# One set in four of a selective scan takes delta*u*B from TensorE; states outside channels; the convolved map is streamed

## The chip, the cores and the metric

The kernel runs on one core of a Trainium2 chip. The metric is the device time of one execution in microseconds (us), lower is better. Three executions of the kernel before took 12178.32, 12185.96 and 12192.31 us. All data are float32.

A NeuronCore has engines that each work through an instruction queue of their own, in order: TensorE (PE, with its weight loads PEld), VectorE (DVE), ScalarE (ACT), GpSimd (POOL) and the sync engine (SP), which issues most DMA transfers. They hand work to each other by semaphores. On-chip data lie in SBUF (128 partitions) and in PSUM (128 partitions, eight banks of 512 float32 a partition).

## The reference, cut to what matters

Two image layers run one after the other on 8 images of 64 x 64 positions and 96 channels. Each is a group norm, an input projection to 192 inner channels and 192 gates, a 3x3 depthwise convolution, a state-space scan with 16 states per inner channel, a norm with a gate, an output projection, and a residual. In the first layer the scan runs in four directions (by row, by column, and both backward):

```python
def _selective_scan(u, delta, A, Bs, Cs, D, delta_bias):
    delta = softplus(delta + delta_bias[None, :, None])
    def step(h, inp):
        u_t, d_t, B_t, C_t = inp        # B_t, C_t: 16 states, the same for all channels
        dA = exp(d_t[..., None] * A)
        h = dA * h + d_t[..., None] * B_e * u_t[..., None]
        return (h, sum(h * C_e, axis=-1))
    _, ys = lax.scan(step, h0, (u_l, d_l, B_l, C_l))
    return moveaxis(ys, 0, -1) + u * D[None, :, None]

xs = _cross_scan(xc)                    # 4 directions of the convolved map xc
x_dbl = einsum('bkdl,kcd->bkcl', xs, x_proj_w)
dts, Bs, Cs = x_dbl[:, :, :R], x_dbl[:, :, R:R+N], x_dbl[:, :, R+N:]
dts = einsum('bkrl,kdr->bkdl', dts, dt_projs_w)
y = _selective_scan(xs, dts, -exp(A_logs), Bs, Cs, Ds, dt_projs_b)
```

So for each channel c, state s and position t the scan needs a decay exp(delta[c,t] A[c,s]), a drive delta[c,t] u[c,t] B[s,t], a linear recurrence over t, and a sum over s of h C[s,t].

## The kernel before, in words

**Tiling.** For each image the first layer's scan is cut into 16 *units*: 4 directions x 4 stretches of T = 1024 positions. A unit has two *jobs*, one for each half of 96 inner channels. A job has three *groups* of 32 channels, and a group has four *sets*, i = 0 to 3, of 4 states. A set is one tile of 128 partitions (32 channels x 4 states) by 1024 positions. That makes 384 sets an image and 3072 in all, 256 jobs of 12 sets. From the second image on, six *short* sets for the other layer (on the ends of the map alone) hang on the end.

**One set** takes these steps. In brackets is the engine and the line:
- `fill` (ACT, L940): the decay, exp(scale * dt), into a PSUM tile of the pool `pslot`, which has two slots.
- `advance_set` (DVE): the product of the group's `drive` (delta*u, copied to PSUM by ACT in L957) and the replicated B (L974), then the recurrence, a tensor_tensor_scan (L987), into a `set` tile. For set i = 3 the product is made early on POOL from SBUF (`early`, L964), and DVE makes the scan alone.
- `keep_state` (ACT, L998): the last column is kept for the next stretch.
- `read_out` (POOL, L1003): `out` = `set` times the replicated C.
- `collect` (PE, L1039): four matmuls by `w_gather` sum the four states into `acc`, one PSUM bank for a group, four quarters of 256 positions on four blocks of 32 partitions. Ahead of set 0, four matmuls (L1030) begin the sums with what `y` holds from the directions before, or with the skip term for the first direction.
- `release` (ACT, L1069): after the group's last set, four copies bring `acc` back to the map `y`. The pool `pacc` has one slot: a group's first matmul waits for the release of the group before.

**The order is written out by hand** in `scan_rows`. A loop over n = the number of the set on DVE issues for each step, in this order: the loads (`fetch` of dt and dtu for the group five sets on, `replicate` of B and C for the unit four sets on), `advance_set(n)`, `keep_state(n-1)`, `fill(n+1)`, `drive(n+2)`, `release(n-4)`, `read_out(n-1)`, `early(n+2)`, `collect(n-3)` and the stages of a *plan* for this step. In the steps with (n+1) % 4 == 0 the stages come before `collect`. The program keeps this order on every engine (`tc.manual_schedule()`).

**The plan** spreads other work over the steps: for the job two ahead, its deltas (`ready_by_time`: matmuls L694 for the argument, ACT for softplus, transposes back by L728, the copy L740, the product delta*u on POOL, L606, and the store to DRAM, L616); for the unit two ahead its projection (L576); and the convolutions of the next image's first layer and of the last image's second (`conv_beside`, L1106). All of these share one PSUM bank (`pmisc`, one slot), so each stage on PE waits for the ACT copy of the stage before.

**Layouts.** In a set, the four states of a channel lie on adjacent partitions (`rep` is loaded by one DMA of 32 channels x 4, with the state index inner). The convolved map `xc` (two tiles of 32 KB a partition in `keep`: this one, and y) stays in SBUF for the whole scan; the next one is written to DRAM by `conv_beside` and loaded by `next_map` in four pieces at the end.

The lines that the change touches most:

Of the kernel before, what the change touches and what calls it, by code (L numbers as in the profile page):

```python
# [16 lines left out]
L = HH * WW  # L17
# [14 lines left out]
HALF = 2 * (T // P) * C  # L32
# [20 lines left out]
def two_ss2d_layers(ctx: ExitStack, tc: tile.TileContext, t: dict, out: bass.AP):  # L53
# [16 lines left out]
    keep = ctx.enter_context(tc.tile_pool(name="keep", bufs=2))  # L70
# [47 lines left out]
    w["skip0"] = const.tile([C, NH, C], F32, name="skip0")  # L118
    for h in range(NH):
        nc.vector.tensor_scalar(  # L120
            w["skip0"][:, h, :], w["eye"], w["dsum0"][:, h : h + 1], None, ALU.mult
        )

# [264 lines left out]

    def like(ap, by_column):

        return ap.rearrange("p (a b) -> p a b", b=HH) if by_column else ap
# [39 lines left out]
    def scan_rows(xc, y, parts, plan, rows, beside):  # L431
# [10 lines left out]
        with (  # L442
            tc.tile_pool(name="loads", bufs=2, side="right") as loads,
            tc.tile_pool(name="piece", bufs=1) as piece,
            tc.tile_pool(name="work", bufs=2) as work,
# [8 lines left out]
            with tc.manual_schedule():  # L454
                state = None
                arena = piece.tile([P, 4 * T], F32, name="arena")
                plan.setdefault(-1, []).insert(0, lambda: low_rows(x_dbl, units[1], rows))
                for n in range(-AHEAD, max(total + 4, max(plan, default=0) + 1)):
                    at = lambda i: sets[n + i] if 0 <= n + i < total else None
                    m, j = divmod(n + 1, PER)  # L460
                    if j == 0 and 0 <= m < len(jobs):

                        stages = []
                        if m + 2 < len(jobs):
                            prepare = short_ready if jobs[m + 2]["unit"]["short"] else ready_by_time
                            stages += prepare(xc, x_dbl, jobs[m + 2], arena, pmisc)
                        if m % NH == 1 and m // NH + 2 < len(units):
                            unit = units[m // NH + 2]
                            project = short_projection if unit["short"] else projection
                            stages += project(xc, x_dbl, unit, rows, pmisc)  # L470
                        for step, stage in stages:
                            plan.setdefault(n + step, []).append(stage)
                    fetch(at(AHEAD), False, loads)
                    fetch(at(2), True, loads)
                    replicate(at(AHEAD_BC), x_dbl, loads)
                    replicate_short(at(AHEAD_BC), "b", loads)
# [5 lines left out]
                    fill(at(1), pslot)  # L482
                    drive(at(2), False, pdrive)
# [6 lines left out]
                    if not late:  # L490
                        collect(at(-3), xc, y, pacc)
                    for stage in plan.pop(n, []):
                        stage()
                    if late:
                        collect(at(-3), xc, y, pacc)
# [23 lines left out]

    def ring(s):  # L520
        return s["unit"].get("ring", 2 * NS + 1)

    def fetch(s, short, loads):
# [1490 lines left out]
```

## Time and profile before

| | |
|---|---|
| three runs | 12178.32 / 12185.96 / 12192.31 us |
| profiled execution, its own time | 12189.28 us |
| its span, first to last instruction | 12187.5 us |
| busy: PE / weight loads / DVE / ACT / POOL | 72% / 33% / 89% / 74% / 86% |
| mean granted TensorE clock | 0.77 |
| DMA | 1862 MB, 153 GB/s on average |
| DVE scans, L987 | x3072, 2344 or 2286 ns each |
| DVE products, L974 | x2352, 1199 ns |
| POOL readout, L1003 / early product, L964 | x3120, 2361 ns / x768, 2414 ns |

A row of the profile names the source line, the engine, the operation, output and inputs by the program's names, the shapes and the count; then the group's busy time in us and the mean of one in ns; then the idle time of the engine just before these instructions, and what ended most of it. The timeline gives start and length in us. Where a row of the stretches between two times is shown, each engine has its busy time and its number of instructions.

### The profile page before, as it was taken

The page shows a single profiled execution, that of the slowest core. Times are in us where ns is not written, and L with a number is a line of the kernel's source. Part 1 is how long each engine was busy: PE and PEld are TensorE (multiplying, and loading weights), DVE is VectorE, ACT ScalarE, POOL GpSimd, SP SyncE. Part 2 cuts the span into 40 slices and gives each one's busy share as a digit, 9 for nine tenths or more (in the row PEclk, how much of TensorE's full clock was granted, in tenths as well). Part 3 has the DMA queues.
Part 4 walks back from the last instruction along what each step waited for, and adds up shares of the span by engine and source line. Part 5 has one row for each costly group of instructions (what it writes and reads, how often), then busy time and mean ns, then how long its engine had stood idle before and what let it go on. Part 6 is the DMA issues. An engine that isn't in the chain of part 4 may idle for free. (4 is left out here: it accounts for less than half of the span.)

```text
span 12187.5 us, 147673 instructions
## 1 busy us (share of the span) xinstructions
PE 8804.0 (72%) x50996; PEld 4018.9 (33%) x50996; DVE 10891.5 (89%) x6819; ACT 9067.0 (74%) x14930; POOL 10497.4 (86%) x4748
## 2 busy tenths in 40 slices
PE   5775577777777777776777777777687776876567
PEld 2332233332333323333233332333233332333222
DVE  6999889997999979999799997999979998899985
ACT  4777777777777777777778777787777777777775
POOL 3999889996999969999699986999879998799973
PEclk7776677778777887778877778777787777877667
DMA  3444444445444444444444444444544444444441
GB/s 96 166 153 156 138 161 155 160 163 153 153 161 164 164 142 165 153 160 160 144 167 163 164 151 155 163 155 160 174 131 165 164 164 156 146 150 158 159 142 59
DMA packets 670707, 1862.42 MB, mean 153 GB/s; under 512 B 186728, under 2 KB 201486, under 8 KB 669949
## 3 DMA queue, kind: packets, MB, share of 16 engines
q1 hardware_dynamic: 662781, 1840.30, 45.4%
q10 hardware_dynamic: 7168, 12.59, 0.3%
q8 instruction: 405, 6.64, 0.2%
q14 instruction: 353, 2.89, 0.1%
HBM read 1539.34 MB, written 313.28 MB: 152 GB/s over the span
## 5 line engine op out<-in xcount | busy, mean ns | idle before, releaser
L1003 POOL TENSOR_TENSOR out<-set,c_rep 128x1024 f32<-128x1024 f32 x3120 | 7305.7, 2361 | 826.4 <-PE acc L1039 329.8
L987 DVE TENSOR_TENSOR_SCAN set<-decay,state,set 128x1024 f32<-128x1024 f32 x2304 | 5360.5, 2344 | 350.5 <-ACT decay L940 112.6
L940 ACT ACTIVATE decay<-dt_rep,w_a 128x1024 f32<-128x1024 f32 x3072 | 3424.0, 1115 | 430.3 <-DVE set L987 428.9
L974 DVE TENSOR_TENSOR set<-drive,b_rep 128x1024 f32<-128x1024 f32 x2352 | 2819.2, 1199 | 26.3 <-ACT drive L957 16.0
L1039 PE MATMUL acc<-out,w_gather 128*32 128x256 f32 x24576 | 2384.5, 516 | 6.8 <-POOL out L1003 6.7
L1106 PE MATMUL ps_conv<-edged,taps 96*96 96x512 f32 (+1 forms) x4032 | 2198.5, 688 | 10.9 <-ACT arena L706 8.3
L964 POOL TENSOR_TENSOR set<-dtu_rep,b_rep 128x1024 f32<-128x1024 f32 x768 | 1853.7, 2414 | 89.5 <-DMA dt_far<-arena 39.1
L987 DVE TENSOR_TENSOR_SCAN set<-decay,set 128x1024 f32<-128x1024 f32 x768 | 1743.0, 2286 | 140.3 <-ACT decay L940 47.9
L728 PE MATMUL ps_sp<-w_eye,arena 128*96 128x128 f32 x7680 | 1162.0, 316 | 712.1 <-ACT arena L740 679.7
L1030 PE MATMUL acc<-map,w_eye 96*32 96x256 f32 x4608 | 577.1, 584 | 1359.0 <-ACT map L1069 1092.3
L1069 ACT COPY map<-acc 32x256 f32<-32x256 f32 x3072 | 1471.3, 479 | 66.2 <-PE acc L1039 25.8
L728 PEld LDWEIGHTS ps_sp<-w_eye,arena 128*96 128x96 f32 x7680 | 1005.7, 147 | 1017.6 <-ACT arena L740 795.1
L1039 PEld LDWEIGHTS acc<-out,w_gather 128*32 128x32 f32 x24576 | 878.3, 140 | 1382.9 <-issue 1072.0
L998 ACT COPY state<-set 128x1 f32<-128x1 f32 x2304 | 433.1, 188 | 1070.4 <-DVE set L987 1062.4
L694 PE MATMUL ps_dt<-w_dtw,x_dbl 7*128 7x96 f32 x3840 | 798.1, 370 | 498.7 <-ACT arena L740 423.1
L1106 PEld LDWEIGHTS ps_conv<-edged,taps 96*96 96x96 f32 (+1 forms) x4032 | 701.3, 189 | 1276.1 <-issue 1186.0
L694 PEld LDWEIGHTS ps_dt<-w_dtw,x_dbl 7*128 7x128 f32 x3840 | 695.3, 267 | 743.6 <-ACT arena L740 496.6
L957 ACT COPY drive<-dtu_rep 128x1024 f32<-128x1024 f32 (+1 forms) x816 | 816.5, 1001 | 33.5 <-DVE x_in L1651 13.5
L705 ACT ACTIVATE arena<-ps_dt 128x384 f32<-128x384 f32 x480 | 235.9, 492 | 620.8 <-PE ps_dt L694 597.4
L1030 PEld LDWEIGHTS acc<-map,w_eye 96*32 96x32 f32 x4608 | 104.1, 125 | 1679.8 <-ACT map L1069 1304.3
L606 POOL TENSOR_TENSOR arena<-arena,map 96x1024 f32<-96x1024 f32 x240 | 635.4, 2647 | 12.0 <-ACT arena L740 12.0
L576 PE MATMUL ps_proj<-map,w_wx 96*78 96x512 f32 x512 | 405.9, 931 | 13.7 <-ACT z L640 9.6
(202 smaller groups left out, 7682.4 us busy)
## 6 DMA issues: line engine op xcount, KB each, us to landing
dt_rep<-dt_far SPq DMA_DIRECT2D x768, 512.0 KB
dtu_rep<-dtu_far SPq DMA_DIRECT2D x768, 512.0 KB
b_rep<-x_dblr SPq DMA_DIRECT2D x256, 512.0 KB
c_rep<-x_dblr SPq DMA_DIRECT2D x256, 512.0 KB
b_rep<-x_dblc SPq DMA_DIRECT2D x256, 512.0 KB
c_rep<-x_dblc SPq DMA_DIRECT2D x256, 512.0 KB
dt_far<-arena SPq DMA_DIRECT2D x240, 384.0 KB
dtu_far<-arena SPq DMA_DIRECT2D x240, 384.0 KB
```

Of the source, the lines that this page charges most:

```text
L694: nc.tensor.matmul(job["ps"][:, j, :], unit["x_dbl"][: R + 1, at : at + P], w["dtw0"][:, k, h * C : (h + 1) * C], start=True, stop=True,)
L728: nc.tensor.matmul(job["ps"][:C, j * P : (j + 1) * P], job[name][:, s * BLOCKS + j, :], w["whole_eye"], is_transpose=True, start=i == 0, s ...
L940: nc.scalar.activation(s["decay"], s["group"]["dt"], AF.Exp, scale=rate)
L957: nc.scalar.copy(s["group"]["drive"], s["group"]["dtu"])
L964: nc.gpsimd.tensor_tensor(s["buf"], s["group"]["dtu"], b, ALU.mult)
L974: nc.vector.tensor_tensor(s["buf"], s["group"]["drive"], b, ALU.mult)
L987: nc.vector.tensor_tensor_scan(ordered(s["buf"], unit), ordered(s["decay"], unit), ordered(s["buf"], unit), 0.0 if unit["nth"] == 0 else s ...
L1003: nc.gpsimd.tensor_tensor(s["out"], s["buf"], s["unit"]["c", s["i"]], ALU.mult)
L1030: nc.tensor.matmul(acc, lhs[:, GC * g : GC * (g + 1)], positions(old[:, h, :], unit["column"], unit["t0"] + at, n), start=True, stop=False ...
L1039: nc.tensor.matmul(acc, w["gather"], s["out"][:, at : at + n], start=False, stop=s["i"] == NS - 1, skip_group_check=True,)
L1069: nc.scalar.copy(yk, like(acc, unit["column"]))
L1106: nc.tensor.matmul(job["ps"][:C, :], taps[l][:k, h, tap, :], edged[:k, tap // 3 : tap // 3 + rows, tap % 3 : tap % 3 + WW], start=tap == 0 ...
```

## The change

**Set 1 of each group on TensorE.** For i = 1 the product with B on DVE goes. TensorE makes delta*u*B straight into a PSUM slot of `pslot`: for each block of 64 positions and each of the four states, delta*u turned (positions on the partitions, 32 channels) is multiplied by a 64 x 64 block that has B on its diagonal and zeros elsewhere. Blocks of the first and second half of the 1024 positions lie on partitions 0 to 63 and 64 to 127, so 8 blocks x 4 states x 2 halves = 64 matmuls write the tile. The scan reads its source from there. The decay of set 1 goes to a tile in SBUF, since the slot is taken.

**The diagonals** are made in DRAM: two buffers are zeroed once, and for each unit four DMAs write the 4 x 1024 values of B, element by element, on the diagonals (`spread_diagonal`, 24 sets ahead). They are loaded in four parts, two DMAs each (`load_diagonal`). B of set 1 is no longer replicated.

**delta*u turned.** `turning` transposes a job's delta*u in eight matmuls and two ACT copies. delta*u is now kept in the order of these blocks, and its store to DRAM takes two DMAs.

**Who multiplies what else.** POOL's early product moves from set 3 of every group to set 0 of the first and third group of a job. DVE multiplies set 0 of the second group, set 2 and set 3.

**States outside.** In a set the four states are now the outer index of the partitions (32 channels, four times), so each replicated load becomes four DMAs of 32 partitions. The ring for B and C has 8 slots in place of 9, dtu has one slot in place of two, and is fetched one step later. `drive` is copied in step n-1 in place of n-2.

**The map is streamed.** The convolved map no longer stays in SBUF: it is stored twice in DRAM, by row and by column (`store_maps`, five DMAs a piece), and each unit loads its 1024 positions (`load_u`). The skip term is made by ACT into `y` (`skip_term`) in place of the first matmuls' weights. `next_map` is gone.

**Steps of the plan.** The deltas' stages stand at other steps by half (`late`), the convolution's nine matmuls are issued three at a time in every job.

The diff, cut to its core:

```diff
+RB = P // 2
+NR = HALF // RB        # 8 blocks of 64 in a half
+BY_PE = 1
+RING = 2 * NS
...
+    def store_maps(b, h, at, v):
+        far, far_col = xc_far[b]
+        nc.sync.dma_start(far[:, h, at], v)
+        rows = slice(at.start // WW, at.stop // WW)
+        for q in range(NT):
+            dst = far_col[:, h, q * T : (q + 1) * T].rearrange("p (a b) -> p a b", b=T // HH)
+            nc.sync.dma_start(dst[:, rows, :], by_piece(v)[:, q])
+    def load_u(b, unit):
+        unit["u"] = upool.tile([C, NH, T], F32, name="u")
+        nc.sync.dma_start(unit["u"], xc_far[b][unit["column"]][:, :, t0 : t0 + T])
+    def skip_term(unit, h, y):
+        nc.scalar.mul(y[:, h, t0 : t0 + T], unit["u"][:, h, :], w["dsum0"][:, h : h + 1])
...
-                    fetch(at(AHEAD), False, loads)
-                    fetch(at(2), True, loads)
+                    fetch(at(AHEAD), ("dt",), False, loads)
+                    fetch(at(AHEAD - 1), ("dtu",), False, loads)
+                    fetch(at(2), ("dt", "dtu", "cum"), True, loads)
                     replicate(at(AHEAD_BC), x_dbl, loads)
+                    spread_diagonal(at(2 * PER), x_dbl)
+                    head = sets[0] if n == -AHEAD else at(2 * NS - 1)
+                    load_diagonal(head, range(1), diagonals)
+                    load_diagonal(at(NS - 1), range(1, PARTS), diagonals)
...
                     advance_set(at(0), state, work)
                     keep_state(at(-1))
-                    fill(at(1), pslot)
-                    drive(at(2), False, pdrive)
+                    product_by_pe(at(1), pslot)
+                    fill(at(1), pslot, work)
+                    drive(at(1), False, pdrive)
                     drive(at(1), True, pdrive)
                     release(at(-4), y, beside)
...
+    def load_channels(rep, src):
+        for s in range(GS):
+            nc.sync.dma_start(rep[GC * s : GC * (s + 1)], src)
...
+    def spread_diagonal(s, x_dbl):
+        for i in range(GS):
+            dst = bass.AP(tensor=whole.tensor, offset=whole.offset + i * RB,
+                ap=[[2 * NR * GS * RB + 1, RB], [GS * RB, 2 * NR], [1, 1]])
+            src = x_dbl[unit["k"] % 2][row + i, unit["t0"] : unit["t0"] + T]
+            nc.sync.dma_start(dst, src.rearrange("(b r) -> r b", r=RB).unsqueeze(2))
...
+    def product_by_pe(s, pslot):
+        s["drive"] = pslot.tile([P, T], F32, name="decay")
+        turned, at = group["job"]["turned"], slice(GC * group["g"], GC * (group["g"] + 1))
+        for b in range(NR):
+            for i in range(GS):
+                for h in range(2):
+                    rows = slice(RB * h, RB * (h + 1))
+                    start = HALF * h + RB * b
+                    nc.tensor.matmul(
+                        s["drive"][GC * i : GC * (i + 1), start : start + RB],
+                        turned[rows, b, at],
+                        s["unit"]["diagonal", b // n][rows, b % n, i, :],
+                        start=True, stop=True, skip_group_check=True)
...
+    def by_pe(s):
+        return s["i"] == BY_PE and not s["unit"]["short"]
     def by_gpsimd(s):
-        return s["i"] == NS - 1
+        return s["i"] == 0 and s["group"]["g"] != 1 and not s["unit"]["short"]
...
+        if by_pe(s):
+            s["decay"] = work.tile([P, T], F32, name="decay_far", bufs=1)
+            nc.scalar.activation(s["decay"], s["group"]["dt"], AF.Exp, scale=rate)
+            return
...
-            b = unit["b", s["i"]]
-            nc.vector.tensor_tensor(s["buf"], s["group"]["drive"], b, ALU.mult)
+            if by_pe(s):
+                source = s["drive"]
+            else:
+                b = unit["b", s["i"]]
+                nc.vector.tensor_tensor(s["buf"], s["group"]["drive"], b, ALU.mult)
+                source = s["buf"]
...
             ordered(s["decay"], unit),
-            ordered(s["buf"], unit),
+            ordered(source, unit),
```

## The prediction

> **What bounds the kernel now.** I read the page's shares first, then the costliest groups, then the busy time of one inner stretch, then the waits and the timeline of one group.
>
> ```profile
> PE 8804.0 (72%) x50996; PEld 4018.9 (33%) x50996; DVE 10891.5 (89%) x6819; ACT 9067.0 (74%) x14930; POOL 10497.4 (86%) x4748
> ...
> L1003 POOL TENSOR_TENSOR out<-set,c_rep 128x1024 f32<-128x1024 f32 x3120 | 7305.7, 2361 | 826.4 <-PE acc L1039 329.8
> L987 DVE TENSOR_TENSOR_SCAN set<-decay,state,set 128x1024 f32<-128x1024 f32 x2304 | 5360.5, 2344 | 350.5 <-ACT decay L940 112.6
> L940 ACT ACTIVATE decay<-dt_rep,w_a 128x1024 f32<-128x1024 f32 x3072 | 3424.0, 1115 | 430.3 <-DVE set L987 428.9
> L974 DVE TENSOR_TENSOR set<-drive,b_rep 128x1024 f32<-128x1024 f32 x2352 | 2819.2, 1199 | 26.3 <-ACT drive L957 16.0
> L964 POOL TENSOR_TENSOR set<-dtu_rep,b_rep 128x1024 f32<-128x1024 f32 x768 | 1853.7, 2414 | 89.5 <-DMA dt_far<-arena 39.1
> L1069 ACT COPY map<-acc 32x256 f32<-32x256 f32 x3072 | 1471.3, 479 | 66.2 <-PE acc L1039 25.8
> ```
>
> Over the whole span DVE is busy 89% and POOL 86%, but that mixes the row scans with the phases between images. The row scan alone, in 1000 us of the second image (busy us of PE, PEld, DVE, ACT, POOL, then clock, DMA share and GB/s):
>
> ```profile
> 1700.00:2700.00 1000.00, 758.03 (x4708) 364.00 (x4706) 963.12 (x553) 775.29 (x1287) 946.51 (x405) 0.78 0.48 165
> ```
>
> DVE has 4% idle and POOL 5%: both bound it, TensorE and ACT do not. Per job (12 sets, three groups of four; 256 jobs) DVE works 12 scans x 2.33 (mean of both forms of L987) + 9 products x 1.20 (L974) + 0.58 for the convolution's curve = 39.3 us, and 96.3% busy makes that 40 to 41 us a job. What TensorE waits for, since it is about to get work that DVE waits for:
>
> ```profile
> PEld acc L1030 <- ACT map L1069: 1572.8, 351, 12.7
> ...
> PE ps_dt L694 <- ACT arena L740: 423.1, 232, 3.1
> ```
>
> TensorE's queue stands behind ACT: the first matmul of a group's accumulation (L1030) waits until ACT has copied the previous group's sums out of the one PSUM bank (L1069). Where in time that lies, at the end of a job (start, length in us):
>
> ```profile
> 2406.64 4.59 DVE L987 TENSOR_TENSOR_SCAN set<-decay,state,set 128x1024 f32<-128x1024 f32 x2
> ...
> 2409.12 1.11 ACT L940 ACTIVATE decay<-dt_rep,w_a 128x1024 f32<-128x1024 f32 x1
> 2410.26 1.49 ACT L1069 COPY map<-acc 32x256 f32<-32x256 f32 x4
> 2411.15 1.20 DVE L974 TENSOR_TENSOR set<-drive,b_rep 128x1024 f32<-128x1024 f32 x1
> 2411.78 0.58 ACT L740 COPY arena<-ps_sp 96x512 f32<-96x512 f32 x1
> ...
> 2412.41 1.13 PE L694 MATMUL ps_dt<-w_dtw,x_dbl 7*128 7x96 f32 x8 [2.20 <-ACT arena L740]
> ...
> 2413.47 0.64 PE L1030 MATMUL acc<-map,w_eye 96*32 96x256 f32 x8
> ...
> 2413.93 1.05 PE L1039 MATMUL acc<-out,w_gather 128*32 128x256 f32 x16
> ```
>
> DVE ends the scan of set 3 at 2411.2 (call this E). ACT's copies end at 2411.75, then its copy L740 frees the shared bank for L694, and only at 2413.5 does TensorE begin the sums. The first set's 16 passes leave it at about 2414.4, E + 3.1 us. Nothing on DVE depends on that today. After the change, the new products stand exactly there.
>
> **What the change removes.** In set 1 of each group DVE's L974 is gone: 3 x 1.20 us a job. Set 3 goes back from POOL to DVE (+3 x 1.20), set 0 goes to POOL in two groups of three (-2 x 1.20). Net -2.40 us on DVE and one L964, -2.41 us, on POOL, a job. Both bounds fall by 6%, so without a new wait a job takes about 36.4 + 0.6 + the present 0.6 of gaps = 37.6 us against 39.9 to 40, and the kernel 256 x 2.4 = 614 us less.
>
> **What it adds to TensorE, and its price P.** 64 products of 64x32 by 64x64 a group; the trace shows two passes for each float32 product (L1039: 3072 sets x 4 products are x24576), so 128 passes. No row has 64-row tiles. The nearest is the gather L1039, four 32-column tiles:
>
> ```profile
> 2425.20:2425.21 0.01, 0.01 (x6) 0.01 (x2) 0.00 (x0) 0.00 (x0) 1.00 0.00 0
> 2425.21:2425.22 0.01, 0.01 (x8) 0.01 (x3) 0.00 (x0) 0.00 (x0) 1.00 0.00 0
> ...
> 2425.20 1.05 PE L1039 MATMUL acc<-out,w_gather 128*32 128x256 f32 x16
> ```
>
> Within 20 ns four passes begin beside four of the line before, under 10 ns apart. The 16 passes make four rounds in 1.05 us less a tail of 0.38, so a round of 256 columns lasts 0.21 us at full clock, and 64 columns 0.053 us. If all eight tiles run together, 16 rounds take 0.85 us at full clock, 1.7 at half, 1.1 at the granted 0.78; with the tail of 0.3, P = 1.4 us. Lower bound 1.1 (full clock). [...]
>
> **Where the products stand.** They write the PSUM slot that the scan of the last group's set 3 reads, so they can't begin before E. And in program order they follow the previous group's first collect, hence the release. Counted from the end of the scan of set 2, which lies E - 3.54 now that set 3 has its product on DVE: ACT's state copy 0.19, decay 1.12, the drive copy 1.00 (L957, moved one step later to this place), release 4 x 0.48 = 1.92: 4.23, that is E + 0.7. Handing over to the first collect takes 1.3 us at mean clock (0.9 in the timeline above at full, 1.7 at half).
> - Into the middle group (its set 0 is on DVE, deadline E + 1.20 + 2.34 = 3.54): 0.7 + 0.1 + 1.3 + 1.4 = E + 3.5. Stall 0, on average 0.3 for the copies by column, which are the slower ones.
> - Into the last group (deadline: scan of set 0 alone, E + 2.34): the same 3.5, stall 1.2.
> - Into the next job: before the collect TensorE has a stage that waits for ACT's L740 (0.58), queued behind the release: then eight passes of L694 (1.66, 798.1 us over 480 bursts) or sixteen of L728 (2.42, 1162 over 480), mean 2.04. 0.7 + 0.1 + 0.58 + 2.04 + 1.3 + 1.4 = E + 6.1, stall 3.75.
> The decay of set 1 now goes to SBUF and doesn't wait for the slot; it is ready at about E + 2 and covered. What is queued behind the stalled scan on DVE is all of the group: the next product (L974) can't pass it; POOL's readout of set 1 and TensorE's gather follow as much later, so POOL (35.7 us a job) is never the bound. Sum a job: stalls 5.25, saved 2.40: +2.85 us, x256 = +730 us.
>
> **The rest.** Eight transposes and two ACT copies (L705's form, 0.49) a job to turn delta*u: about 1 us on each, beside the scans; it costs nothing unless ACT gets late, since they come after the release. The skip term: 64 ACT products at 1.14 (L1725's form), once in four jobs, hidden alike. Transfers: diagonals 1 MB a unit in place of 0.5 MB of B, the map read 16 times 768 KB an image instead of four and stored twice: about +165 MB (128 x 0.52 + 96 x 0.79 + 7 x 3.1) on 1862, with a DMA share of 0.48 hidden. SP issues 102 transfers a unit in place of some 30, at 0.31 (delta stores) to 0.57 us (broadcasts): 32 to 58 us of a unit's 86, so hidden on average; at unit borders, where 46 of them fall into five sets, I take 0.2 us a unit. Start (zeroed diagonals, 40 stores of the map) and seven phases between images: +40 us, an estimate from 40 stores x 0.35 and some 3 us for the later turning in each phase. Together +65.
>
> Sum on the profiled execution: 12187.5 + 730 + 65 = 12,982; what lies around the span is 1.8 us (its own time 12189.3), and the median shown, 12186, is 3 us below that. Predicted 12,980 us. Its own range, with P from 1.1 to 2.2 and the other links at full or half clock: 12,450 to 13,600.
>
> **Rivals.**
> - The cover holds (faster). If release and stages get out of TensorE's way, so that the products start near E, P = 1.4 fits into 2.34 and the stall goes. For it: the saving is real on both bounds, and stalls give ACT and TensorE time to catch up. Against: the wait of L1030 for L1069 above. With stalls of 1.0 us a job, -1.4 x 256 = -360: 11,830. It decides once the three stalls together stay under 2.4 us. Chance 0.16.
> - [...] Chance 0.14.
> - SP becomes the new wait: three times the issues, each in order behind waits for POOL and DVE. 5 us a unit more, x128: 13,600. Against: 58 us of 86 at worst. Chance 0.10.
> - It moves nothing: stalls eat exactly the saving, 12,190. Chance 0.03.
> - The forecast case: 0.57.
>
> **How the numbers follow.** Within 0.2% (24 us) is about what can't be told from no change for this kernel. Faster 0.16 and slight tails of the main case 0.01; same 0.03; slower 0.80. The range 11,900 to 14,200 leaves out about half of the first rival and most of the second (0.17).
>
> **What the profile after would show.** Right: the scan of set 1 (from `decay_far`) with idle before it released by the PE products, about 1350 us in all, longest at the start of a job; DVE busy about 79%; L974 at x1840 (7 a job and the 48 short sets) in place of x2352; the products' 128 passes in 1.1 to 1.7 us. Wrong: if that idle time is small, if the burst takes 3 us, if DVE waits for transfers of b_rep or the diagonals instead, or if the release ends before E as a rule.

## The result, and the profile after

The changed kernel takes 14754.4 us (median of 4 runs, 14752.5 to 14761.9) against 12189.1 us of the kernel before beside it (12178.3 to 12195.0): 1.2107 times as long, 95% interval 1.2086 to 1.2128. That is 2565 us slower. Slower was the forecast, but by 794 us, and 14,754 lies above the range given.

The page of the changed kernel, its busy line and the groups that answer to those shown of before (L1151 is the scan now, L1167 POOL's readout, L1137 the product on DVE, L1193 the start of a group's sums, L666 the new products):

```profile
PE 10308.8 (70%) x151348; PEld 5185.0 (35%) x151348; DVE 10315.8 (70%) x6305; ACT 9385.2 (64%) x15506; POOL 9947.6 (67%) x4493
...
L1167 POOL TENSOR_TENSOR out<-set,c_rep 128x1024 f32<-128x1024 f32 x3120 | 7359.9, 2362 | 3740.4 <-DVE set L1151 1681.5
...
L1151 DVE TENSOR_TENSOR_SCAN set<-decay_far,state,decay 128x1024 f32<-128x1024 f32 x576 | 1351.8, 2347 | 2111.0 <-PE decay L666 2054.4
...
L1137 DVE TENSOR_TENSOR set<-drive,b_rep 128x1024 f32<-128x1024 f32 x1840 | 2209.1, 1201 | 249.9 <-ACT drive L1117 151.9
L1193 PE MATMUL acc<-map,w_eye 96*32 96x256 f32 x6144 | 773.9, 589 | 1814.0 <-ACT map L1232 1411.2
L666 PE MATMUL decay<-diagonal,turned 64*32 64x64 f32 x98304 | 1434.8, 277 | 142.2 <-DMA diagonal<-diagonal 102.9
...
L1151 DVE TENSOR_TENSOR_SCAN set<-decay_far,decay 128x1024 f32<-128x1024 f32 x192 | 439.0, 2287 | 766.5 <-PE decay L666 758.9
```

DVE and POOL do 576 and 550 us less work (the forecast had some 615 on each), yet no engine is full any more: the busiest is at 70%. The scan of set 1 (its decay comes from `decay_far`) has 2878 us of idle time before it: 2111 in the row with a carried state, 767 in that of the first unit of each direction. In the row scan (same columns as the stretch shown of before) every engine's busy time has fallen:

```profile
2200.00:3200.00 1000.00, 728.83 (x11789) 380.97 (x11788) 746.03 (x413) 651.66 (x1079) 730.85 (x311) 0.80 0.63 150
```

The end of a job in the timeline, the place that the forecast took for the worst:

```profile
3018.72 4.59 DVE L1151 TENSOR_TENSOR_SCAN set<-decay,state,set 128x1024 f32<-128x1024 f32 x2
3019.69 1.49 ACT L1232 COPY map<-acc 32x256 f32<-32x256 f32 x4
3021.21 0.58 ACT L889 COPY arena<-ps_sp 96x512 f32<-96x512 f32 x1
3021.84 1.13 PE L843 MATMUL ps_dt<-w_dtw,x_dbl 7*128 7x96 f32 x8 [3.28 <-ACT arena L889]
...
3022.90 0.64 PE L1193 MATMUL acc<-map,w_eye 96*32 96x256 f32 x8
...
3023.97 2.05 PE L666 MATMUL decay<-diagonal,turned 64*32 64x64 f32 x128
...
3026.14 2.35 DVE L1151 TENSOR_TENSOR_SCAN set<-decay_far,state,decay 128x1024 f32<-128x1024 f32 x1 [2.83 <-PE decay L666]
```

The chain is link for link the one forecast: release L1232, copy L889 of the shared bank, stage L843, first collect L1193, products L666, scan. It explains part of the loss only, and the experiments show where the rest is.

Two measures are used below. *Excess* is a kernel's median less that of the kernel before measured beside it (which took 12,159 to 12,189). *Set periods* are worked out from the trace: the time from the end of one full scan to the end of the next, averaged by place in the unit (24 sets) over all eight images, row units. Where sums over all units are given, they are worked out from the same ends of scans, in the profiled executions.

### The profile page after: what moved, and what is told of

It is laid out like the page before. It is cut to its first block, busy times and chain, and to the rows that moved or that the text cites. A ratio compares the mean times of both kernels' runs of the same rounds, so it can differ in the third digit from the quotient of the medians.

```text
span 14752.0 us, 363543 instructions
## 1 busy us (share of the span) xinstructions
PE 10308.8 (70%) x151348; PEld 5185.0 (35%) x151348; DVE 10315.8 (70%) x6305; ACT 9385.2 (64%) x15506; POOL 9947.6 (67%) x4493
## 3 DMA queue, kind: packets, MB, share of 16 engines
q8 instruction: 1190, 19.50, 0.6%
## 5 line engine op out<-in xcount | busy, mean ns | idle before, releaser
L1167 POOL TENSOR_TENSOR out<-set,c_rep 128x1024 f32<-128x1024 f32 x3120 | 7359.9, 2362 | 3740.4 <-DVE set L1151 1681.5
L1151 DVE TENSOR_TENSOR_SCAN set<-decay,state,set 128x1024 f32<-128x1024 f32 x1728 | 4033.0, 2345 | 176.4 <-ACT decay L1100 41.0
L1100 ACT ACTIVATE decay<-dt_rep,w_a 128x1024 f32<-128x1024 f32 x2304 | 2570.9, 1116 | 411.2 <-DVE set L1151 362.5
L1151 DVE TENSOR_TENSOR_SCAN set<-decay_far,state,decay 128x1024 f32<-128x1024 f32 x576 | 1351.8, 2347 | 2111.0 <-PE decay L666 2054.4
L1137 DVE TENSOR_TENSOR set<-drive,b_rep 128x1024 f32<-128x1024 f32 x1840 | 2209.1, 1201 | 249.9 <-ACT drive L1117 151.9
L1193 PE MATMUL acc<-map,w_eye 96*32 96x256 f32 x6144 | 773.9, 589 | 1814.0 <-ACT map L1232 1411.2
L666 PE MATMUL decay<-diagonal,turned 64*32 64x64 f32 x98304 | 1434.8, 277 | 142.2 <-DMA diagonal<-diagonal 102.9
L666 PEld LDWEIGHTS decay<-diagonal,turned 64*32 64x32 f32 x98304 | 1267.7, 130 | 689.7 <-issue 566.2
L1232 ACT COPY map<-acc 32x256 f32<-32x256 f32 x3072 | 1463.8, 476 | 47.5 <-PE acc L1202 7.3
L1151 DVE TENSOR_TENSOR_SCAN set<-decay,set 128x1024 f32<-128x1024 f32 x576 | 1311.5, 2286 | 203.8 <-POOL set L1124 101.6
L1124 POOL TENSOR_TENSOR set<-dtu_rep,b_rep 128x1024 f32<-128x1024 f32 x512 | 1237.0, 2416 | 211.0 <-DMA dtu_rep<-dtu_far 98.9
L843 PE MATMUL ps_dt<-w_dtw,x_dbl 7*128 7x96 f32 x3840 | 659.6, 320 | 680.6 <-ACT arena L889 514.9
L1151 DVE TENSOR_TENSOR_SCAN set<-decay_far,decay 128x1024 f32<-128x1024 f32 x192 | 439.0, 2287 | 766.5 <-PE decay L666 758.9
L1193 PEld LDWEIGHTS acc<-map,w_eye 96*32 96x32 f32 x6144 | 144.4, 130 | 2220.1 <-ACT map L1232 1598.5
```

Of the source, the lines that this page charges most:

```text
L666: nc.tensor.matmul(s["drive"][GC * i : GC * (i + 1), start : start + RB], turned[rows, b, at], s["unit"]["diagonal", b // n][rows, b % n, ...
L1100: nc.scalar.activation(s["decay"], s["group"]["dt"], AF.Exp, scale=rate)
L1124: nc.gpsimd.tensor_tensor(s["buf"], s["group"]["dtu"], b, ALU.mult)
L1137: nc.vector.tensor_tensor(s["buf"], s["group"]["drive"], b, ALU.mult)
L1151: nc.vector.tensor_tensor_scan(ordered(s["buf"], unit), ordered(s["decay"], unit), ordered(source, unit), 0.0 if unit["nth"] == 0 else s[" ...
L1167: nc.gpsimd.tensor_tensor(s["out"], s["buf"], s["unit"]["c", s["i"]], ALU.mult)
```

## The experiments

**1. How much is the products' wait?** Three edits that only move instructions.

*Products a step earlier*, ahead of the stages and of the first collect:

```diff
-                    product_by_pe(at(1), pslot)
                     fill(at(1), pslot, work)
+                    product_by_pe(at(2), pslot)
```

> The changed kernel with one move: the 64 products are issued one step earlier, ahead of the plan's stages and of the first collect, which now follow them on TensorE. Position theory (the products are late because they stand behind the release, the stage and the first collect): they start as the scan of set 3 ends (E), end at E + 2.0, within both deadlines (2.34 and 3.54), so DVE's wait for them falls from 2813 us to under 300 and the time to 11,900-12,400 (stages and collects, now 2 us later, take some of it back). Length theory (the burst of 1.9 us itself is what DVE waits for, since its slot is free only at E): the wait falls by no more than a half, 13,300 or more. Transfer theory (the streamed map, the split loads and the diagonals set the pace): 14,300 or more.

*The release at the head of its step*:

```diff
+                    release(at(-4), y, beside)
                     advance_set(at(0), state, work)
...
-                    release(at(-4), y, beside)
```

> The changed kernel with ACT's release at the head of its step, ahead of the decay of the next set 0 and of the drive copy (2.1 us of ACT work). Position theory: the first collect starts up to 2 us earlier where the release is what it waits for (the last group, half of the first and of the third), DVE's wait falls by about 1.0-1.5 us a group: 13,600-14,000. Length theory and transfer theory: no change, 14,600-14,800.

*The first collect of a group behind the products* (the stages stay ahead):

```diff
+                    wait = lambda s: s and s["i"] == 0 and not s["unit"]["short"]
+                    if wait(at(-4)):
+                        collect(at(-4), y, pacc)
                     late = (n + 1) % NS == 0
...
-                    if late:
+                    if late and not wait(at(-3)):
                         collect(at(-3), y, pacc)
```

> The changed kernel with the first collect of each group moved behind the products (one step later), the stages of the plan still ahead of them. Position theory: the products into the last group start at E (stall 3.2 to 0), those into the middle group wait for the convolution alone (3.0 to about 1), those into the next job still wait for the stage behind the release (5.1 to about 2.5): 11.3 to 3.5 us a job, 12,700-13,000. If the stages are the whole matter and not the collect: 14,000 or more. Transfer theory: 14,500 or more.

| kernel | median, us | ratio to before (interval) | excess | DVE's wait for the products |
|---|---|---|---|---|
| changed | 14754.4 | 1.2107 (1.2086 to 1.2128) | 2565 | 2813 us, 735 times |
| products a step earlier | 13895.7 | 1.1416 (1.1397 to 1.1435) | 1729 | 565 us, 152 times |
| release first | 13930.1 | 1.1448 (1.1429 to 1.1467) | 1763 | 1437 us, 430 times |
| first collect behind | 13994.1 | 1.1499 (1.1480 to 1.1518) | 1827 | 1124 us, 274 times |

All three give back 740 to 840 us, and none comes near the kernel before. Of what was expected if the place of the products is the whole matter, only the second run came out (13,600 to 14,000); the first and third lie 1500 and 1000 us above. The first takes 2250 us off the wait and gets 836 for it. What DVE waits for in the changed kernel, and then with the products a step earlier (total, times, longest in us):

```profile
DVE set L1151 <- PE decay L666: 2813.3, 735, 8.9
...
DVE set L1137 <- ACT drive L1117: 151.9, 105, 7.3
DVE set L1151 <- ACT decay L1100: 115.5, 46, 7.1
```

```profile
DVE set L1151 <- PE decay L666: 564.7, 152, 7.6
DVE set L1151 <- ACT decay_far L1089: 425.9, 319, 4.5
DVE set L1151 <- ACT decay L1100: 385.6, 339, 7.2
DVE set L1137 <- ACT drive L1117: 318.6, 194, 3.2
```

Other waits take its place: something else was late at the same time.

**2. The change without products.** POOL makes the product of set 0 in all three groups, DVE that of sets 1 to 3; there are no diagonals. Everything else stays: states outside channels, loads in four, the streamed map, the turning (used by nothing), the moved plan.

```diff
-        return s["i"] == BY_PE and not s["unit"]["short"]
+        return False
...
-        return s["i"] == 0 and s["group"]["g"] != 1 and not s["unit"]["short"]
+        return s["i"] == 0 and not s["unit"]["short"]
...
-RING = 2 * NS
+RING = 2 * NS + 1
```

> The changed kernel without the products and the diagonals: DVE multiplies set 1 by B again, POOL makes set 0 in all three groups (so that DVE and POOL have the work of the kernel before), B is replicated again; the streamed map, the states outside with four loads in place of one, and the turning of delta*u stay. Position and length theories: all but the phases between images comes back, 12,190 + some 200 = 12,300-12,600. Transfer theory: most of the loss stays, above 13,500.

13541.9 us, ratio 1.1123 (1.1105 to 1.1142), excess 1375. More than half of the loss has nothing to do with TensorE's products. The page of this kernel (L1135 is DVE's product, L1122 POOL's, L1115 the copy of delta*u to PSUM):

```profile
L1135 DVE TENSOR_TENSOR set<-drive,b_rep 128x1024 f32<-128x1024 f32 x2352 | 2824.7, 1201 | 466.0 <-DMA b_rep<-x_dblc 168.0
...
L1122 POOL TENSOR_TENSOR set<-dtu_rep,b_rep 128x1024 f32<-128x1024 f32 x768 | 1854.5, 2415 | 512.2 <-DMA dtu_rep<-dtu_far 348.1
...
L1115 ACT COPY drive<-dtu_rep 128x1024 f32<-128x1024 f32 (+1 forms) x816 | 816.6, 1001 | 494.8 <-DMA dtu_rep<-dtu_far 381.0
```

Before, DVE's product had 26 us of idle time ahead of it and POOL's 90. Now they wait for transfers of B and delta*u. The set periods tell where (us, first ten sets of a unit; a set whose product POOL makes takes 2.2, another 3.6):

| set | 1 | 2 | 3 | 4 | 5 | 6 | 7 | 8 | 9 | 10 |
|---|---|---|---|---|---|---|---|---|---|---|
| before | 3.56 | 3.57 | 3.57 | 3.15 | 3.57 | 3.56 | 3.56 | 2.23 | 3.57 | 4.07 |
| changed, without products | 2.24 | 3.62 | 3.79 | 6.04 | 5.14 | 3.57 | 3.56 | 4.07 | 2.29 | 3.59 |

Summed over all units, the first eight sets of a unit take 773 us more than before, most of it in the fourth and fifth. There SP sends eight loads of B and C, each now four DMAs, beside those of delta and delta*u. That is not all: the middle eight sets take 22 us less, but the last eight 423 us more, and 188 us lie outside the scans. In the seventeenth and eighteenth set DVE waits 253 us for ACT's decays, before 70; in the twentieth and twenty-first it waits for POOL's readout (107 us) and for a convolution copy on ACT (81). This second loss has nothing to do with how the loads are cut: it is 403 to 432 us in all runs of experiments 4 and 5 that leave out the products, and -4 us in experiment 6. The stages of the plan that the change moved may be its cause; no run tests that.

**3. One DMA a load.** The same bytes in the same layout, with the count of states as the outer step of the source; once on the changed kernel, once without products, once also with two buffers for delta*u.

```diff
-        for s in range(GS):
-            nc.sync.dma_start(rep[GC * s : GC * (s + 1)], src)
+        nc.sync.dma_start(rep, src.unsqueeze(0).broadcast_to([GS, *src.shape]))
...
-                load_states(rep, src)
+                nc.sync.dma_start(rep, src.unsqueeze(1).broadcast_to([GS, GC, T]))
```

and for the two buffers, which come back in experiment 5:

```diff
-                    fetch(at(AHEAD), ("dt",), False, loads)
-                    fetch(at(AHEAD - 1), ("dtu",), False, loads)
+                    fetch(at(AHEAD), ("dt", "dtu"), False, loads)
...
-                    rep = loads.tile([P, T], F32, name=f"{c}_rep", bufs=2 if c == "dt" else 1)
+                    rep = loads.tile([P, T], F32, name=f"{c}_rep", bufs=2)
```

> The changed kernel with each replicated load of dt, delta*u, B and C sent as one DMA of 512 KB again instead of four of 128 KB (same bytes, same layout; the short sets' B and C stay split). Queue theory: SP issues 14,406 DMAs in 7,062 us of the changed kernel against 4,232 in 2,145 before; at a unit's start 32 quarter loads of B and C stand ahead of the next delta*u. One DMA in four gives back 4 to 6 us per unit, 500 to 800 us: about 14,050. Transfer theory (the 16 DMA engines, busy 57%, and the short packets are what is late): the same packets, so within 100 us of 14,754. Stage theory (what is late is ScalarE's and TensorE's own stages): within 100 us of 14,754.

> The changed kernel without products and diagonals (GpSimd makes all of those sets) and with one DMA per load. Without products it took 13,542; per unit its DVE was 8 to 9 us longer than before, most of it in the fourth and fifth set of a unit (6.0 to 6.9 and 5.1 us against 3.2 and 3.6), which wait for delta*u. Queue theory: 12,650 to 12,950. Transfer theory: 13,450 to 13,550. Stage theory: about 13,400.

> As the one before (no products, one DMA per load), and delta*u has two buffers and is fetched with dt again, five sets ahead, as in the kernel before. What is left of the change: layout, streamed map, turning, the moved plan. Queue theory: the single buffer's part comes back too, 12,400 to 12,700, at least 150 less than with one buffer. Transfer theory: 13,400. Stage theory: within 50 us of the run with one buffer.

19719.6, 18740.5 and 18467.8 us, ratios 1.62, 1.54 and 1.52: every theory missed. The stretches where a unit starts, of the second kernel (the last two numbers are DMA share and GB/s):

```profile
7220.80:7230.80 10.00, 5.09 (x44) 2.98 (x36) 4.13 (x3) 3.03 (x5) 9.19 (x4) 0.78 0.26 105
7230.80:7240.80 10.00, 6.12 (x8) 2.25 (x9) 3.41 (x3) 2.00 (x4) 2.34 (x1) 0.53 0.26 103
```

A share of 0.26 is four of 16 DMA engines (0.26 of 16 is 4.2). With states outermost a single load has an outer step of 4, a quarter load one of 32, and with quarter loads the share at a unit's start is 1.05, with 239 GB/s (the kernel of experiment 2, from 5249.17 us on, shown further below). That the outer step sets the number of engines is the author's reading; no run changes it alone. So these runs say nothing on the count of DMAs. They show what the cut in four avoids: a share of 0.26.

**4. Without products, and without the column-ordered copy** of the convolved map (column units read the row-ordered copy, so their data are wrong).

```diff
-        for q in range(NT):
-            dst = far_col[:, h, q * T : (q + 1) * T].rearrange("p (a b) -> p a b", b=T // HH)
-            nc.sync.dma_start(dst[:, rows, :], by_piece(v)[:, q])
...
-        src = xc_far[b][unit["column"]]
+        src = xc_far[b][0]
```

> The changed kernel without products and diagonals, loads in four as it has them, and the column-ordered copy of the convolved map is not stored; column units read the row-ordered copy (their data are wrong, the amounts read are the same). This takes away 480 DMAs with packets of 64 bytes, about 0.9 of 1.6 million packets. Transfer theory: these short packets hold up the loads, 500 us or more come back: 13,000 or less. Queue theory: they take SP 340 us in all, behind them waits little: 13,350 to 13,500. Stage theory: 13,540.

13364.1 us, ratio 1.0987 (1.0969 to 1.1005), excess 1202: this copy and its 64-byte packets cost 173 us, not the 500 or more of one theory. The fourth set still takes 5.3 us.

**5. Whole loads with 16 source rows, at the price of more stored bytes.** B and C are stored four times in DRAM, so that a load has 16 source rows and covers 128 partitions in one DMA; then the same as four DMAs over every fourth partition (`rep[j:P:GS]`, j = 0 to 3, with two partitions for each source row); then on the changed kernel as it is; then with the products a step earlier and the release first.

```diff
+                for kk in range(2):
+                    copies = x_dbl[2 + k % 2][2 * N * GS * kk :, t0 : t0 + T][: 2 * N * GS, :]
+                    src = unit["x_dbl"][ROWS * kk + R + 1 : ROWS * (kk + 1), :]
+                    nc.sync.dma_start(
+                        copies.rearrange("(n r) t -> n r t", r=GS),
+                        src.unsqueeze(1).broadcast_to([2 * N, GS, T]),
+                    )
...
-                load_states(rep, src)
+                nc.sync.dma_start(rep, src.unsqueeze(1).broadcast_to([GS * GS, P // GS // GS, T]))
```

> The changed kernel without products and diagonals, and each row of B and C is stored four times in DRAM (two more stores per projected unit), so that a load of four states is again one DMA over 128 partitions with 16 source rows, each read by 8 partitions. The quarter loads of delta and delta*u stay. Where a unit starts the run without products moved 4 KB packets of 280 ns (159 before) on 16 busy engines, 240 GB/s against 392: the quarter loads, into 32 partitions each, are the suspect. Theory: packets near 160 to 200 ns at the unit's start, the fourth and fifth set come back to 3.6 to 4.3 us from 6.0 and 5.1, 4 us or more per unit: 12,900 to 13,100 against 13,542. Rival (what is late is the single buffer of delta*u and the moved stages, whatever the packets cost): 13,400 or more.

> As the one before, but every load of B and C is four DMAs of 32 partitions again, over every fourth partition (0, 4, 8 and so on) instead of 32 neighbours: the same count of DMAs and the same packets as the changed kernel's, other partitions. [...] If it is the number of DMAs (SP's issue of 0.4 to 0.5 us each), it goes back to 13,400 or more.

> The changed kernel as it is, products and all, with only the four stored copies and the single loads of B and C. Theory: the same 4 us per unit come back in part, since the products' wait fills some of the same time: 14,200 to 14,500. Rival: within 100 us of 14,754.

> All that helped together: four copies with single loads of B and C, the products issued one step earlier ahead of the stages, and the release at the head of its step. Alone the early products gave 860 us and the early release 825 of the 2,565 lost; the loads of a unit's start are the floor under both. Expected 13,000 to 13,400; below 12,190, faster than the kernel before, only if nothing but the loads stood behind those floors.

| kernel | median, us | ratio (interval) | excess |
|---|---|---|---|
| no products, whole loads of B and C | 13604.9 | 1.1175 (1.1150 to 1.1200) | 1424 |
| no products, quarters over every fourth partition | 13800.4 | 1.1334 (1.1304 to 1.1365) | 1620 |
| changed, whole loads of B and C | 14946.7 | 1.2284 (1.2252 to 1.2316) | 2766 |
| the same, products earlier, release first | 14083.6 | 1.1564 (1.1538 to 1.1590) | 1903 |

Nothing came back, where 450 us or more were expected. The second kernel differs from the first in the cut of B's and C's loads alone, and is 196 us slower, although its 4 KB packets are the quicker ones: 180 ns against 278 (medians of the unit starts, from 12 us before to 15 us behind the end of the unit before). So the cut does cost something in this layout. The last kernel is even slower than with the products earlier alone (13895.7). Then the same for delta and delta*u, so that no quarter load is left (delta*u in straight order, one store less), and with two buffers for delta*u:

```diff
-                nc.sync.dma_start(far, job[c])
+            for g in range(NG):
+                dst = far[P * g : P * (g + 1), :].rearrange("(s c) t -> c s t", s=GS)
+                src = job[c][GC * g : GC * (g + 1), :]
+                nc.sync.dma_start(dst, src.unsqueeze(1).broadcast_to([GC, GS, T]))
...
-                load_channels(group[c], src)
+                    nc.sync.dma_start(group[c], src)
```

> The changed kernel without products and diagonals; the rows of B, C, delta and delta*u are all stored four times in DRAM, so that every long load is one DMA of 512 KB over 128 partitions on 16 engines, with no quarter loads left; delta*u stays in straight order (one store of its kind less; what the turning then takes is in the wrong order and used by nothing). Theory that both limits of a unit's start bind together: packets near 160 to 200 ns there, fourth and fifth set of a unit near 4 us, 12,700 to 13,000. Rival (single buffer of delta*u, moved stages): 13,300 or more, with the fourth set still above 5.5 us.

> As the one before, and delta*u has two buffers and is fetched with delta five sets ahead. What is left of the change: the streamed map with its stores and loads, the turning, the moved stages of the plan. If the single buffer is what is late, 300 us or more faster than with one; if only transfers were late, within 100 us of it. What stays above 12,190 is the moved stages and the streamed map: 12,400 to 12,700.

13523.2 us (1.1119, 1.1099 to 1.1138; excess 1364) and 13338.3 us (1.0974, 1.0955 to 1.0992; excess 1179). The second buffer gives 185 us, where 300 were expected of it; whole loads alone give nothing. In the latter the first eight sets of the units still take 481 us more than before, so the cut is not all that is late there. But this remedy changes a second thing. A stretch of 1000 us inside the row scan of the first of the two:

```profile
5000.00:6000.00 1000.00, 729.99 (x4220) 338.80 (x4219) 838.48 (x489) 705.17 (x1221) 814.11 (x352) 0.75 0.76 209
```

The DMA engines are busy 76% of the time, against 48% before: 2643 MB move instead of 1862. One queue was relieved and another filled. The next run adds no byte.

**6. The kernel before, with its long loads cut in four.** Each load of delta, delta*u, B and C becomes four DMAs over every fourth partition. Packets, bytes and layout are as before.

```diff
-                nc.sync.dma_start(group[c], src.unsqueeze(1).broadcast_to([GC, GS, n]))
+                for j in range(GS):
+                    nc.sync.dma_start(rep[j:P:GS, :n], src)
...
-                nc.sync.dma_start(rep, src.unsqueeze(0).broadcast_to([GC, GS, T]))
+                for j in range(GS):
+                    nc.sync.dma_start(rep[j:P:GS], src[j : j + 1].broadcast_to([GC, T]))
```

> The kernel before, with each long load of delta, delta*u, B and C cut into four DMAs of 128 KB over every fourth partition: the same bytes and packets, about 6,100 DMAs more for SP. If SP's issue alone is a limit at a unit's start (32 quarter loads of B and C take 16 us where 8 whole ones took 5), 300 us or more slower than before: 12,500 to 12,800. If SP has room, within 60 us of 12,190.

13296.3 us, ratio 1.0934 (1.0916 to 1.0952), excess 1137: more than twice the 300 us from which SP was to count as a limit. SP's queue around the start of a unit, start and length in us; first before, then cut in four:

```profile
4687.60 1.22 SPq L534 DMA_DIRECT2D dt_rep<-dt_far  x1
4688.92 0.54 SPq L534 DMA_DIRECT2D dtu_rep<-dtu_far  x1
4689.51 0.60 SPq L544 DMA_DIRECT2D b_rep<-x_dblr  x1
...
4697.13 0.51 SPq L534 DMA_DIRECT2D dtu_rep<-dtu_far  x1
4698.48 0.51 SPq L544 DMA_DIRECT2D b_rep<-x_dblr  x1
4699.76 0.51 SPq L544 DMA_DIRECT2D c_rep<-x_dblr  x1
```

```profile
5125.47 3.14 SPq L535 DMA_DIRECT2D dt_rep<-dt_far  x4
5128.71 2.45 SPq L535 DMA_DIRECT2D dtu_rep<-dtu_far  x4
5131.20 2.50 SPq L546 DMA_DIRECT2D b_rep<-x_dblr  x4
...
5150.41 2.50 SPq L535 DMA_DIRECT2D dtu_rep<-dtu_far  x4
5153.01 2.45 SPq L546 DMA_DIRECT2D b_rep<-x_dblr  x4
5155.56 2.45 SPq L546 DMA_DIRECT2D c_rep<-x_dblr  x4
```

In these rows a DMA mostly costs SP 0.5 to 0.6 us (the first load of before 1.2), whether it moves 512 KB or 128. Before, the twelve loads around a unit's start leave SP in 12.7 us (4687.6 to 4700.3). Cut in four they take 32.5 us (5125.5 to 5158.0), almost without a pause, while DVE needs 3.6 for a set. The fourth set of a unit then takes 9.4 us in place of 3.15, all other places nearly what they were (4.52 in the third set at most), a unit 87.0 us in place of 79.6. Here the 16 DMA engines are not full, in the stretch in which DVE works 1.6 us of ten:

```profile
5149.35:5159.35 10.00, 5.01 (x11) 1.55 (x9) 1.58 (x1) 4.33 (x8) 1.74 (x1) 0.84 0.64 184
```

A 4 KB packet takes 159 ns (median of the whole run), the same as before. So the cut, through SP's issue alone, costs the kernel before 1137 us, 1054 of them in the first eight sets of the units. SP's total busy time tells nothing of it: 7113 us of 13,302, or 53%. It is no measure of the cut's part in the changed layout: there the same eight sets lose 773 us, and the packets are slower.

**7. The same queue, relieved in the changed layout.** Without products, the quarter loads of C go out from ACT's queue.

```diff
-                load_states(rep, src)
+                load_states(rep, src, nc.scalar if c == "c" else nc.sync)
```

> The changed kernel without products and diagonals (13,542), and the quarter loads of C, 16 a unit, are issued by ScalarE's queue instead of SP's. Same bytes, same packets. SP theory: at a unit's start 16 x 0.55 = 9 us leave SP's queue, and delta*u comes earlier; ScalarE pays 8 us of its own there, so 200 to 500 us come back: 13,050 to 13,350. Packet theory (4 KB packets of 280 ns on 16 full engines set the pace): within 100 us of 13,542, or slower for ScalarE's part.

14840.3 us, ratio 1.2189 (1.2169 to 1.2210), excess 2672: far slower, where 200 to 500 us were to come back. Idle time of the engines that use delta*u, by what ended it: first with all loads on SP, then with C's on ACT; and what DVE waits for in the latter.

```profile
  DMA dtu_rep<-dtu_far: 729.1, 183
```

```profile
  DMA dtu_rep<-dtu_far: 1.9, 1
```

```profile
DVE set L1149 <- ACT decay L1098: 2257.7, 1015, 29.9
```

The wait for delta*u is gone, from 729 us to 2, and the fourth set takes 3.67 us instead of 6.04. That looks like a relieved queue, but it is not shown. From a unit's first load of B to the end of the issue of its second group's delta*u, 25.9 us pass on average with C on ACT and 23.7 without (SP issues during 11.0 and 16.4 of them): delta*u does not leave sooner after the loads begin. What changed is DVE, which is late itself: the first set of a unit takes 7.3 us in place of 2.2. The price is on ACT: its DMAs take 0.31 us each and follow each other every 1.1 us (medians), and the decays that DVE needs stand behind them. So this run does not tell how much SP's queue costs in the changed layout.

## Why the prediction was right in direction and wrong in size

The 2565 us are 1190 for the products (2565 less 1375) and 1375 for all else. The forecast had +730 for stalls less savings, and +65 for all else. By place, the profiled executions give 773 us in the first eight sets of the units, 423 in the last eight and 188 outside the scans, less 22 in the middle. The column-ordered copy is 173 of them. The cut in four cost 1137 in the kernel before; its share in the changed kernel was not separated.

- **What bounds the kernel, what the change removes:** right. DVE's products fell from x2352 to x1840 as named, DVE to 70% where 79% was named.
- **Where the products stand:** right as a mechanism. The idle time before the scan of set 1 is released by L666, longest at the start of a job. It is 2878 us in the two rows of that scan, against some 1350 named.
- **The sizes of the stalls:** too small. The 2878 us are 11.2 us a job, where 5.25 was forecast. By place: into the middle group 3.1 us in row units and 3.3 in column units (0.3 forecast), into the last 2.7 and 3.6 (1.2), into the next job 4.5 and 5.3 (3.75). Three terms were mis-sized. P has a median of 1.95 us, not 1.4: bursts at a granted clock of 1.00 take 1.48 us, those at 0.50 take 2.05, and seven in ten begin at 0.50. Even at full clock a round of eight passes takes some 78 ns (burst at 5744.39 us), not 53. From the start of the first collect to that of the products it takes 1.4 to 1.9 us, not 1.3. And into the middle group a convolution stage on TensorE can stand ahead of the products: it does in all 62 of these 256 groups whose stall is over 5 us; the longest is 8.9. Yet the net cost of the products is about 1190 us, 4.7 a job against 2.85 forecast, for part of the stalls falls where the kernel is late anyway: in the second group of a unit, where the change without products already loses 437 us, the products add 19, in the fourth, where it loses nothing, 410. It may also be why taking 2250 us off this wait gave 836.
- **The price P:** the trace decided for the gather row as its measure. Eight passes of a burst, on tiles of 64 x 32, begin within 47 ns (median of the 768 bursts). The second rival (chance 0.14) rested on a P of more than twice the forecast's 1.4 us, and no run shows it: the median is 1.95 us, and 742 of the 768 bursts stay under 3 us. So this rival falls, though the time came out above the one that it gave. The 2.2 us at the end of the range for P are not a measured term either; 727 of the bursts are shorter.
- **The rest, the step that failed:** "SP issues 102 transfers a unit in place of some 30 ... so hidden on average; at unit borders, where 46 of them fall into five sets, I take 0.2 us a unit". This whole term, +65 us, measured 1375. At the units' starts it is 6.0 us a unit (773 over 128) against 0.2. The average, 58 of 86 us, was near enough (SP is busy 7062 us of 14,752 in the changed kernel), but the loads of B and C are not spread over the unit. They leave in one row, and delta*u, which the next group needs, stands behind or among them. Five sets last 18 us; 46 issues at the 0.57 us that the forecast itself used are 26. That sum was not made. The cut alone, in the kernel before, costs 8.9 us a unit. Two smaller parts were put too low as well: 188 us outside the scans against 40, and 423 us in the last eight sets of the units against nothing, where DVE waits for ACT; of the turning on ACT the forecast had said that it costs nothing "unless ACT gets late".
- **The rivals:** "SP becomes the new wait" named the right place, with 5 us a unit against 6.0 (of which SP's share is open), and was wrong in standing as an alternative: it comes on top of the stalls. Both together as forecast would have given 13,620, still some 1130 below the result. "The cover holds" falls with the stalls; even with the products moved ahead the kernel stays 14% above the kernel before.

What stays open: how much of the 773 us at the units' starts is SP's issue. A second limit lies close to it. At a unit's start, first before, then in the changed kernel without products:

```profile
4699.21:4709.21 10.00, 9.33 (x70) 5.72 (x69) 9.23 (x5) 7.74 (x16) 6.04 (x3) 0.68 1.01 392
```

```profile
5249.17:5259.17 10.00, 8.69 (x63) 6.04 (x64) 9.26 (x6) 6.48 (x12) 6.36 (x4) 0.66 1.05 239
```

The 16 engines are full in both, but move 392 GB/s and 239: a 4 KB packet takes 159 ns before and 284 here (medians of the unit starts). What makes them slower is not shown. The author's guess is that it is the 32 neighbouring partitions into which a quarter load goes. For it speak the quarters over every fourth partition (medians of 180 ns in experiment 5 and 159 in experiment 6); against it, that packets of loads that stood alone ran at 162 ns or less in a quarter of the cases (median 185), and that in the run with whole loads alone the median is 247 ns at the unit starts. How much of the changed kernel's unit start belongs to the slower packets, no run separates. Untested too are the moved stages of the plan behind the 423 us.

## What to carry to other kernels

An issuing queue is to be summed over the few sets in which a burst must leave, with what stands behind the burst, and not over the period: in experiment 6 SP was busy 53% of the time, and the cut cost 1137 us. A layout in which a load takes four DMAs has its price in issues, in experiment 6 mostly 0.5 to 0.6 us each, for 128 KB as for 512. And before costing the new work, it pays to take it out and time what is left of the change.

## What had not been expected of the hardware

- Single loads with an outer step of 4 kept four of the 16 DMA engines busy at a unit's start (experiment 3): share 0.26, 103 GB/s, and the kernel up to 1.62 times as long.
- Eight 64 x 32 tiles of TensorE run together: eight passes begin within 47 ns, and the 128 passes of 64 columns take 1.48 us at a granted clock of 1.00, 2.05 at 0.50 (changed kernel).
- DMAs issued from ACT's queue cost more than their own time of 0.31 us each (experiment 7): 16 a unit moved there added 1297 us, with DVE waiting 2258 us for ACT's decays.
